# Cross-attention and ternary FFN on one core: order of the first loads, of the first batches' attention and of the first weights

## The chip, the cores and the metric

The kernel runs on one core of one Trainium2 chip. The metric is the time of one execution in microseconds (us). Engines are called as in the profile: PE (TensorE), DVE (VectorE), ACT (ScalarE), POOL (GpSimd) and SP (SyncE, which only issues transfers here). PEld is PE's weight load. Times given as "at 16.50" count from the start of the profiled span.

## The reference

Eight batches of 256 tokens, each token 256 wide, all in float32. Each batch has a context of 120 rows.

```python
x = x + xattn(layernorm(x), ctx)              # scores = xn @ ctx.T, gelu(scores) * scores, @ ctx
h = silu((xn2 @ w1.T) * w1_s) * ((xn2 @ w2.T) * w2_s)     # xn2 = layernorm(x), 256 -> 1024
h = gelu((h @ h1.T) * h1_s)                   # 1024 -> 1024
h = gelu((h @ h2.T) * h2_s)                   # 1024 -> 1024
out = x + (h @ w3.T) * w3_s                   # 1024 -> 256
```

The five weight matrices hold only -1, 0 and 1; the scales are per output column.

## The kernel before

**Tiling.** Tokens are taken in four groups of 512 (t = 0 to 3), two batches (b = 2t, 2t + 1) in each. A batch is two blocks of 128 tokens. Products with ternary weights are run on float32r operands split into a high and a low part, so each appears twice. The two hidden layers use a seven-product scheme on quarter matrices.

**Attention** (`Attention.run`, one call for each batch; batch 0 in two calls of one block each, batch 1 and later in one call of two blocks). Its steps, with their lines: load of x (L212) and of the context (L218) on SP; statistics (L245) and their aggregate (L249) on DVE, for batches 0 and 1 also an addition (L251); the reciprocal root on POOL (L256); the norm (L267 on DVE for batches 0 and 1, L264 on ACT later); transposes on PE (L279) and their copy on ACT (L294); scores on PE (L284); an activation made of L297 (ACT), L298 (DVE), L300 (ACT), L302 (DVE); values on PE (L289); the residual sum (L305, DVE), which SP stores to memory (L420). Then the second layer norm by the same lines, transposes (L279), and the split into the high part (L412, ACT) and the low part (L413, DVE) of the tile xT.

**First FFN layer** (`gated`). For each t, eight groups m of eight products (L443) with the weights w12 and xT, followed by a Silu (L464, ACT) and a product with the other side (L466, DVE). For t = 0 it is run in two halves: first the columns of batch 0 alone (256 wide), then those of batch 1. A group takes its PSUM bank in turn from five: for the first half, bank 1, 2, 3, 4, 0 and so on.

**Weights.** w12 comes in two transfers of 1 MB, issued by POOL (L612), for groups m = 0 to 3 and 4 to 7. They read the key `("first", 0, 0)`, which POOL's root of block 0 of batch 0 writes, so they stand behind it. The hidden layers' weights come later (L355). Loads L379 to L388 check that all weights are exactly representable; a branch at the end takes a general version if not. Only that branch reads `sc_half` and `sc_glu`, which `scales` computes (L619, L620).

**Zero matmuls.** Ahead of everything stand 72 matmuls on zeros (L598, `IDLE = 72`) that write bank 4 and keep PE occupied while the first data arrive. They carry a very low priority. The fourth group of the first layer (m = 3) writes the same bank, so it has to follow all 72.

**Order.** Every step is added to a `Plan` with an engine, a cost, and the keys that it reads (`r`) and writes (`w`). A transfer is added as the issuing step and a step on a model of the DMA engines, with a `lag` until it lands. `chain` puts steps with the same name one behind the other, without a wait between them. The planner computes for each step the longest way to the end, changes a few of these ranks at random for each seed in `PICKS`, and runs a list schedule over the modelled engines. The resulting order is written out: on each engine the instructions then run strictly in that order, each waiting for its own inputs. `hold` adds keys that the first statistics of a batch must wait for.

Of the kernel before, what the change touches and what calls it, by code (L numbers as in the profile page):

```python
# [31 lines left out]
RING = 3  # L32

PICKS = (
    24, 34, 68, 75, 109, 200, 234, 262, 306, 335, 347, 388, 480, 484, 636, 688, 746, 771, 875,
    891, 941, 969, 1092, 1139, 1225, 1283, 1374, 1478, 1505, 1565, 1721, 1792, 1831, 1887, 1946,
    2002, 2028, 2205, 2327, 2434, 2594, 2622, 2698, 2823, 3117, 3852, 3875, 4460, 4870, 4887,
    5689, 8901, 9951, 10170, 10586, 11026, 11996, 12028, 14291, 14841, 14964, 15189, 15290,
    15347, 15386, 15476, 15843, 16236,
)  # L40
ALIGN, ALIGN_W3, ALIGN_RIGHT = 16, 8, 112
IDLE = 72
# [27 lines left out]
class Plan:  # L70
# [6 lines left out]
    def add(self, engine, weight, emit, r=(), w=(), lag=None, early=0.0, chain=None):  # L77
        i, deps = len(self.ops), {}
        if lag is None:
            lag = LAG.get(engine, 0.1)  # L80
        for k in r:
            if k in self.writer:
                deps[self.writer[k]] = True
            self.readers.setdefault(k, []).append(i)
        for k in w:
            if k in self.writer:
                deps[self.writer[k]] = True
            for j in self.readers.pop(k, ()):
                if j != i:
                    deps[j] = True  # L90
            self.writer[k] = i
        if chain is not None:
            if chain in self.last:
                deps.setdefault(self.last[chain], False)
            self.last[chain] = i
        self.ops.append((engine, weight, emit, deps, lag, early))
# [74 lines left out]
PE = 0.12  # L171
# [4 lines left out]
def xattn_ffn_kernel(ctx: ExitStack, tc: tile.TileContext, x, ctx_b, wall, scal, s3, out):  # L176
# [6 lines left out]
    sc = const.tile([P, 32], F32, name="sc")  # L183
# [8 lines left out]
    class Attention:  # L192
# [12 lines left out]
        def load(self, plan, b, pieces):  # L205
            i = b % self.loads
            xv = x[b * S : (b + 1) * S, :].rearrange("(j p) d -> p j d", p=P)

            gate = [("first", b - 3, 0)] if b >= 3 else []

            def load_x(js):
                nc.sync.dma_start(self.xb[i][:, js, :], xv[:, js, :])  # L212

            for js in pieces:
                plan.dma("SP", 0.45, lambda js=js: load_x(js), 0.128 * (js.stop - js.start),
                         lag=(2.2, 3.0, 5.0, 6.0, 6.0)[b] if b < 5 else 4.0, r=gate,
                         w=[("xb", i, j) for j in range(js.start, js.stop)])
            plan.dma("SP", 0.45, lambda: nc.sync.dma_start(self.cb[i], ctx_b[b]), 0.25,  # L218
                     lag=(3.0, 3.5, 5.0, 6.0, 6.0)[b] if b < 5 else 4.0, r=gate, w=[("cb", i)])

        def run(self, plan, b, js, bank, bank_key, x1, x1_key, finish, early, hold=()):


            blocks = range(js.start, js.stop)
            nj = len(blocks)
            n = nj * P
            cols = slice(js.start * P, js.stop * P)
            i, il = b % self.n, b % self.loads
            keys = lambda name: [(name, il if name == "xb" else i, j) for j in blocks]
# [3 lines left out]
            xnT, e, q = self.xnT[i][:, :, cols], self.e[i][:, cols], self.q[i][:, cols]  # L233
# [6 lines left out]
            add = plan.add  # L240
# [46 lines left out]
            def values():  # L287
# [4 lines left out]
            layernorm(xb, keys("xb") + list(hold), "first")  # L292
            add("PE", 0.22 * nj, transposes, keys("xn"), [bank_key])
            add("ACT", act(2 * n), lambda: nc.scalar.copy(xnT, halves), [bank_key], keys("xnT"))  # L294
            add("PE", 0.215 * nj, scores, keys("xnT") + [("cb", il)], [bank_key])

            add("ACT", act(n), lambda: nc.scalar.activation(e, g, AF.Square), [bank_key], keys("e"))  # L297
            add("DVE", dve(n), lambda: nc.vector.scalar_tensor_tensor(  # L298
# [2 lines left out]
                [], keys("q"))  # L301
            add("DVE", dve(n), lambda: nc.vector.scalar_tensor_tensor(  # L302
                e, q, 1.0, e, op0=ALU.add, op1=ALU.mult), keys("q"), keys("e"))
            add("PE", 0.215 * nj, values, keys("e") + [("cb", il)], [bank_key])
            add("DVE", dve(2 * n), lambda: nc.vector.scalar_tensor_tensor(  # L305
                x1, y, 0.5, xb, op0=ALU.mult, op1=ALU.add), [bank_key] + keys("xb"), x1_key)
            layernorm(x1, x1_key, "second")
# [8 lines left out]
    with ExitStack() as es, ExitStack() as wide:  # L316
# [18 lines left out]
        xT = [[early_pool.tile([P, 2, N], F32R, name=f"xT{i}{j}") for i in range(2)] for j in range(2)]  # L335
        later = {}

        plan = Plan()
        add = plan.add
# [63 lines left out]
        def attention(b, pieces, banks, early):  # L403
            t, c, i = b // 2, b % 2, b % att.loads
            att.load(plan, b, pieces)
            for js, bank in zip(pieces, banks):
                cols = slice(c * S + js.start * P, c * S + js.stop * P)
                xkey = [("xT", t % 2, c, j) for j in range(js.start, js.stop)]

                def finish(p, bank_key, n, early, cols=cols, xkey=xkey):  # L410
                    hi, lo = (v[:, :, cols] for v in xT[t % 2])
                    add("ACT", act(2 * n), lambda: nc.scalar.copy(hi, p), r=[bank_key], w=xkey)  # L412
                    add("DVE", dve(2 * n), lambda: nc.vector.tensor_sub(lo, p, hi.bitcast(F32)),  # L413
                        r=[bank_key], w=xkey, early=early)

                x1 = att.xb[i][:, js, :]
                x1_key = [("xb", i, j) for j in range(js.start, js.stop)]
                att.run(plan, b, js, mm[bank], ("mm", bank), x1, x1_key, finish, early,
                        [("xT", 0, 0, j) for j in range(2)] if b in (2, 3) else ())
                plan.dma("SP", 0.45, lambda js=js, x1=x1: nc.sync.dma_start(  # L420
                    x1s[b * S : (b + 1) * S, :].rearrange("(j p) d -> p j d", p=P)[:, js, :], x1),
                    0.13 * (js.stop - js.start), r=x1_key,
                    w=[("x1s", 2 * b + j) for j in range(js.start, js.stop)], lag=4.0)
# [181 lines left out]
        add("ACT", 1.3, lambda: nc.scalar.preload_act_table(AF.Silu), w=["table"], early=400.0)  # L605
        plan.dma("SP", 0.4, lambda: nc.sync.dma_start(sc, scal), 0.016, w=["sc"])
        attention(0, one, (5, 6), 20.0)
        attention(1, both, (7,), 10.0)
        plan.dma("SP", 0.4, lambda: nc.sync.dma_start(s3b, s3.partition_broadcast(P)), 0.13, w=["s3b"])

        def load_w12(c):
            nc.gpsimd.dma_start(w12[:, c : c + 2, :], wall[c : c + 2].rearrange("c p f -> p c f"))  # L612

        for c in (0, 2):
            plan.dma("POOL", 0.8, lambda c=c: load_w12(c), 1.05, r=[("first", 0, 0)],
                     w=[("w12", c), ("w12", c + 1)], chain="weights")

        def scales():
            nc.vector.tensor_scalar_mul(sc_half, sc[:, 0:8], 0.5)  # L619
            nc.vector.tensor_mul(sc_glu, sc_half, sc[:, 8:16])  # L620

        add("DVE", 0.4, scales, r=["sc"], w=["scales"])

        def open_middle():

# [19 lines left out]
        for t in range(1, NT):  # L645
            for b in (2 * t, 2 * t + 1):
                attention(b, both, (5 + (b + 1) % 3,), 6.0)
            for js in (range(2), range(2, 4)) if t < HALVED else (range(4),):
                gated(t, js)
# [8 lines left out]
            later["w3"], wall[20:22].rearrange("c p f -> p c f")), 1.05, r=["later"], w=["w3"],  # L658
            chain="weights", lag=4.0)
        add("ACT", 1.3, lambda: nc.scalar.preload_act_table(AF.Gelu), w=["table"])  # L660
        low, high = (0, 1, 2, 3), (4, 5, 6, 7)
        blocks = [(0, 2, 1, 3), (4, 6, 5, 7)]
        spare = (8, 9)
# [34 lines left out]
    with tc.If(inexact == 0 if FORCE_GENERAL else inexact != 0):  # L698
        with ExitStack() as es:
# [8 lines left out]
            for c in range(NCH):  # L708
                w = wpool.tile([P, 1024], F32, tag=f"g{c}", name=f"g{c}")
# [3 lines left out]
            xT = gbuf.tile([P, 2, S], F32, name="xTg")  # L713
            x1 = gbuf.tile([P, 2, D], F32, name="x1g")
            bank = ppa.tile([P, N], F32, name="gpa")
            for b in range(NB):
                plan = Plan()
# [82 lines left out]
```

## Time and profile before

| | |
|---|---|
| median of 3 runs | 334.45 us (334.01 to 334.62) |
| profiled execution | 334.16 us, its span 332.4 us |
| busy: PE, DVE, ACT, POOL | 324.3, 254.9, 211.6, 54.3 us |
| granted clock of PE, mean | 0.995 |
| transfers | 32.44 MB |

The span runs from the first to the last instruction; the execution has some time around it. The chain that ended last follows the work back from the last instruction, at each step to what released it, or to the instruction ahead on the same engine. The timeline gives, for each line: start, length, engine, line, operation, tiles and shapes, count, and in brackets how long the engine was idle before it and what ended that. A busy PE counts the whole length of a matmul, although the next one starts before its end; the distance between starts is what one costs.

### The profile page before, as it was taken

Reading aid. Unit: us, or ns where it says so; the run is one execution under the profiler, and the core shown is the slowest. Engines: PE = TensorE matmul, PEld = TensorE weight load, DVE = VectorE, ACT = ScalarE, POOL = GpSimd, SP = SyncE. Lnnn points to the kernel's source line nnn. Section 1 sums busy time; section 2 is a strip of 40 time slices with the busy share of each in tenths; the row PEclk is TensorE's granted clock in tenths of the full one; section 3 lists DMA queues with packets and bytes.
Section 4 is the critical chain, followed back from the end, with each engine's and each line's share of the span. In section 5 each row is a group of like instructions: output and inputs, shape, how many; then the busy total and the mean of one; then the engine's idle time right before and its main releaser. Section 6 shows DMA issues by size and latency. Waiting matters only on the chain.

```text
span 332.4 us, 4572 instructions
## 1 busy us (share of the span) xinstructions
PE 324.3 (98%) x1678; PEld 275.7 (83%) x1678; DVE 254.9 (77%) x403; ACT 211.6 (64%) x308; POOL 54.3 (16%) x93
## 2 busy tenths in 40 slices
PE   8999999999999999999999999999999999999992
PEld 6899988888888888888888888888888888899991
DVE  4877999878997549978469999928999426738982
ACT  2367776468398867766769755887865657656500
POOL 4164251020024211111123200141100000000000
PEclk9999999999999999999999999999999999999998
DMA  7989710030079494418849650084500000003432
GB/s 194 330 306 344 230 64 2 32 95 3 0 219 103 44 142 95 98 35 194 217 94 239 63 140 0 0 86 47 59 1 2 0 0 2 0 0 98 128 127 73
DMA packets 22382, 32.44 MB, mean 98 GB/s; under 512 B 1744, under 2 KB 15184, under 8 KB 22352
## 3 DMA queue, kind: packets, MB, share of 16 engines
q0 software_dynamic: 10256, 17.30, 27.7%
q1 hardware_dynamic: 12096, 14.77, 14.3%
q8 instruction: 15, 0.25, 0.3%
q14 instruction: 15, 0.12, 0.1%
HBM read 33.64 MB, written 4.19 MB: 114 GB/s over the span
## 4 chain that ended last, share of the span: by engine, by line
PE 96%; DMA 1%; DVE 1%; SPq 0%; issue 0%; ACT 0%
PE mm L519 61%; PE mm L443 18%; PE mm L565 9%; PE mm L279 2%; PE mm L284 2%; PE mm L289 2%; PE mm L598 2%; DMA xb<-x_d 1%; DVE ln_st L245 0%; DVE o L312 0%; DVE o L313 0%; SPq L218 0%; SPq L212 0%; ACT xT L412 0%; DVE xn L267 0%
## 5 line engine op out<-in xcount | busy, mean ns | idle before, releaser
L519 PE MATMUL mm<-hi,w 128*128 128x512 f32 x448 | 119.7, 389 | 0.0
L519 PE MATMUL mm<-lo,w 128*128 128x512 f32 x448 | 119.7, 389 | 0.0
L492 DVE TENSOR_TENSOR lo<-q,hi 128x1024 fp32r<-128x1024 f32 x72 | 85.7, 1219 | 38.3 <-ACT hi L488 38.2
L519 PEld LDWEIGHTS mm<-hi,w 128*128 128x128 f32 x448 | 84.1, 188 | 17.5
L519 PEld LDWEIGHTS mm<-lo,w 128*128 128x128 f32 x448 | 84.1, 188 | 17.5
L488 ACT CAST hi<-q 128x1024 fp32r<-128x1024 f32 x72 | 72.3, 1046 | 10.1 <-PE mm L565 8.8
L443 PE MATMUL mm<-xT,w 128*128 128x512 f32 (+1 forms) x320 | 64.7, 355 | 0.1
L443 PEld LDWEIGHTS mm<-xT,w 128*128 128x128 f32 x320 | 51.8, 189 | 8.0 <-ACT xT L412 0.4
L538 ACT ACTIVATE q<-q,sc 128x512 f32<-128x512 f32 x48 | 34.1, 721 | 22.2 <-DVE q L534 22.1
L528 ACT COPY q<-mm 128x512 f32<-128x512 f32 x48 | 28.1, 586 | 24.0 <-PE mm L519 23.7
L534 DVE TENSOR_TENSOR q<-q,mm 128x512 f32<-128x512 f32 x48 | 32.5, 682 | 12.0 <-PE mm L519 10.8
L381 POOL DMA_DIRECT2D d<-wall_d x22 | 24.5, 1121 | 101.7 <-ACT d L379 98.5
L511 DVE TENSOR_TENSOR q<-q,q 128x1024 f32<-128x1024 f32 x32 | 38.3, 1216 | 0.0
L464 ACT ACTIVATE q<-mm,sc 128x512 f32<-128x512 f32 (+1 forms) x40 | 24.0, 600 | 16.1 <-PE mm L443 16.1
L466 DVE SCALAR_TENSOR_TENSOR q<-q,sc,mm 128x512 f32<-128x512 f32 (+1 forms) x40 | 25.1, 630 | 4.7 <-ACT q L464 2.4
L379 ACT ACTIVATE d<-w 128x1024 bf16<-128x1024 f32 x22 | 23.2, 1057 | 1.6 <-DVE bad L383 1.6
L363 DVE TENSOR_TENSOR w<-w,w 128x512 fp32r<-128x512 f32 x32 | 20.8, 681 | 0.0
L565 PE MATMUL mm<-w,hi 128*128 128x256 f32 x128 | 20.1, 279 | 0.0
L565 PE MATMUL mm<-w,lo 128*128 128x256 f32 x128 | 20.1, 279 | 0.0
L565 PEld LDWEIGHTS mm<-w,hi 128*128 128x128 f32 x128 | 17.3, 188 | 0.1
L565 PEld LDWEIGHTS mm<-w,lo 128*128 128x128 f32 x128 | 17.2, 188 | 0.0
L538 ACT ACTIVATE q<-mm,sc 128x512 f32<-128x512 f32 x16 | 11.0, 687 | 8.2 <-PE mm L519 8.2
(50 smaller groups left out, 197.7 us busy)
## 6 DMA issues: line engine op xcount, KB each, us to landing
w<-wall_d POOLq DMA_DIRECT2D x11, 1024.0 KB, 7.3
d<-wall_d POOLq DMA_DIRECT2D x22, 256.0 KB, 6.3
w<-wall_d SPq DMA_DIRECT2D x8, 512.0 KB, 3.8
x<-x1s SPq DMA_DIRECT2D x16, 128.0 KB, 2.4
out_d<-o SPq DMA_DIRECT2D x16, 128.0 KB, 1.8
cb<-ctx_d SPq DMA_DIRECT2D x8, 248.0 KB, 4.6
xb<-x_d SPq DMA_DIRECT2D x7, 256.0 KB, 4.4
x1s<-xb SPq DMA_DIRECT2D x7, 256.0 KB, 2.4
```

The lines of the kernel that those rows point to most:

```text
L381: plan.dma("POOL", 0.8, lambda: nc.gpsimd.dma_start(d4, src, accum_op=ALU.add), 1.04, w=[("d", i)], lag=8.0)
L443: nc.tensor.matmul(sides[side], lhsT=w12[:, m // 2, (((m % 2) * 2 + side) * 2 + k) * P :][:, :P], rhs=xT[t % 2][i][:, k, cols], start=firs ...
L464: add("ACT", act(n, 1), lambda o=o, b0=b0, m=m: nc.scalar.activation(o, b0, AF.Silu, scale=sc[:, m : m + 1]), r=[("mm", banks[0]), "sc", " ...
L466: add("DVE", dve(n) + 0.05, lambda o=o, b1=b1, m=m: nc.vector.scalar_tensor_tensor(o, o, sc[:, 8 + m : 9 + m], b1, op0=ALU.mult, op1=ALU.m ...
L488: nc.scalar.copy(slot_views(i)[0][:, ms], q[src][:, ms])
L492: nc.vector.tensor_sub(l[:, ms], q[src][:, ms], h[:, ms].bitcast(F32))
L511: add("DVE", dve(1024), lambda ms=ms: nc.vector.tensor_tensor(q[into][:, ms], q[x][:, ms], q[y][:, ms], op=ALU.subtract), r=q_keys(x, ms) ...
L519: nc.tensor.matmul(mm[bank], lhsT=w[:, m, k, :], rhs=part[:, k, :], start=(p in OPENS and kind == 0 and k == 0), stop=(p in CLOSES and kin ...
L528: add("ACT", act(512), lambda: nc.scalar.copy(q[i][:, m], mm[bank]), r=[key], w=[("q", i, m)])
L534: add("DVE", dve(512), lambda: nc.vector.tensor_tensor(o(), o(), mm[bank], op=ALU.add), r=[key], w=[("q", i, m)])
L538: add("ACT", act(512, 1), lambda: nc.scalar.activation(o(), src(), AF.Gelu, scale=sc[:, col : col + 1]), r=["sc", "table"] + ([] if p in a ...
L565: nc.tensor.matmul(mm[banks[j]][:, :D], lhsT=part[:, k, j * P : (j + 1) * P], rhs=later["w3"][:, r, k * D : (k + 1) * D], start=(r == 0 an ...
```

## The change

- The loads of x and context of batches 0 and 1 get the chain `loads`: both blocks of batch 0, its context, then batch 1. Their modelled lags become shorter.
- `run` takes a second list, `hold_values`, which is added to what the values step reads. The statistics of batch 1 are held until POOL's root of block 1 of batch 0 (`("first", 0, 1)`), its values until block 1's part of xT is written.
- The two loads of w12 read `("first", 0, 1)` instead of `("first", 0, 0)`.
- `scales` reads the key `later`, written where the tiles of the hidden layers' second pool are opened, and is added after the loading of the Gelu table.
- The planner's PE cost of scores and values is doubled, and the list `PICKS` is another, of 61 seeds instead of 68.

```diff
 PICKS = (
-    24, 34, 68, 75, 109, 200, 234, 262, 306, 335, 347, 388, 480, 484, 636, 688, 746, 771, 875,
...
+    24, 34, 68, 74, 98, 161, 181, 212, 226, 262, 369, 407, 428, 476, 490, 556, 637, 719, 750,
...
             gate = [("first", b - 3, 0)] if b >= 3 else []
+            chain = "loads" if b < 2 else None
...
                 plan.dma("SP", 0.45, lambda js=js: load_x(js), 0.128 * (js.stop - js.start),
-                         lag=(2.2, 3.0, 5.0, 6.0, 6.0)[b] if b < 5 else 4.0, r=gate,
+                         lag=(1.5, 2.5, 5.0, 6.0, 6.0)[b] if b < 5 else 4.0, r=gate, chain=chain,
                          w=[("xb", i, j) for j in range(js.start, js.stop)])
             plan.dma("SP", 0.45, lambda: nc.sync.dma_start(self.cb[i], ctx_b[b]), 0.25,
-                     lag=(3.0, 3.5, 5.0, 6.0, 6.0)[b] if b < 5 else 4.0, r=gate, w=[("cb", i)])
-
-        def run(self, plan, b, js, bank, bank_key, x1, x1_key, finish, early, hold=()):
+                     lag=(1.8, 3.0, 5.0, 6.0, 6.0)[b] if b < 5 else 4.0, r=gate, chain=chain, w=[("cb", i)])
+
+        def run(self, plan, b, js, bank, bank_key, x1, x1_key, finish, early, hold=(), hold_values=()):
...
-            add("PE", 0.215 * nj, scores, keys("xnT") + [("cb", il)], [bank_key])
+            add("PE", 0.43 * nj, scores, keys("xnT") + [("cb", il)], [bank_key])
...
-            add("PE", 0.215 * nj, values, keys("e") + [("cb", il)], [bank_key])
+            add("PE", 0.43 * nj, values, keys("e") + [("cb", il)] + list(hold_values), [bank_key])
...
-                        [("xT", 0, 0, j) for j in range(2)] if b in (2, 3) else ())
+                        {1: [("first", 0, 1)], 2: [("xT", 0, 0, 0), ("xT", 0, 0, 1)],
+                         3: [("xT", 0, 0, 0), ("xT", 0, 0, 1)]}.get(b, ()),
+                        [("xT", 0, 0, 1)] if b == 1 else ())
...
         for c in (0, 2):
-            plan.dma("POOL", 0.8, lambda c=c: load_w12(c), 1.05, r=[("first", 0, 0)],
+            plan.dma("POOL", 0.8, lambda c=c: load_w12(c), 1.05, r=[("first", 0, 1)],
                      w=[("w12", c), ("w12", c + 1)], chain="weights")
...
-        add("DVE", 0.4, scales, r=["sc"], w=["scales"])
...
         add("ACT", 1.3, lambda: nc.scalar.preload_act_table(AF.Gelu), w=["table"])
+        add("DVE", 0.4, scales, r=["sc", "later"], w=["scales"])
```

## The prediction

> **What bounds the kernel now.** I read the page first, then the chain of waits that ended last, then the timeline of the first 17 us, then the landings of the weights. From the page:
>
> ```profile
> span 332.4 us, 4572 instructions
> PE 324.3 (98%) x1678; PEld 275.7 (83%) x1678; DVE 254.9 (77%) x403; ACT 211.6 (64%) x308; POOL 54.3 (16%) x93
> PE 96%; DMA 1%; DVE 1%; SPq 0%; issue 0%; ACT 0%
> L598 PE MATMUL mm<-zeros 128*128 128x256 bf16 x72 | 11.5, 307 | 1.2 <-DVE zeros L593 1.2
> ```
>
> TensorE (PE) is busy 324.3 of 332.4 us. Of the 8.1 us that are left, 1.15 lie before its first instruction and 6.7 behind its last product (325.64 to 332.4), so almost nothing lies between. Among its work are 72 matmuls on zeros (L598), which compute nothing. Now the chain in order of time (start, length):
>
> ```profile
> 1.65 2.57 DMA xb<-x_d
> 4.25 0.44 DVE ln_st L245
> 5.08 0.33 DVE xn L267
> 5.90 0.76 PE mm L598 x7
> 12.55 1.97 PE mm L598 x18
> 15.82 0.23 PE mm L279 x2
> 16.07 0.38 ACT xT L412
> 16.50 4.32 PE mm L443 x32
> 92.64 203.12 PE mm L519 x896
> 295.75 29.88 PE mm L565 x256
> ```
>
> The first real products (L443) start at 16.50, released by the second block of batch 0. From there on PE issues without a pause worth naming: 203.12 us for 896 products are 0.2267 each, from end to end of the hidden layers. Before 16.50 the zero matmuls fill whatever the attention leaves free, at 0.76/7 = 0.109 us each. That decides how the change must be priced. All 72 are still issued, since the fourth group of first-layer products writes bank 4 behind the last of them. An earlier attention chain therefore doesn't shorten PE's queue; it only exchanges what stands where in it. **The end moves by two things alone: waits of PE that vanish, and waits of PE that appear.**
>
> The timeline shows where batch 0 loses time, and the waits of the weight loads (PEld) what there is to win:
>
> ```profile
> 4.30 0.90 POOL L612 DMA_DIRECT2D w<-wall_d  x1
> 5.21 0.62 POOL L256 TENSOR_TENSOR ln_rs<-ln_ve,eps_exp 128x1 f32<-128x1 f32 x1
> 5.45 0.20 PEld L279 LDWEIGHTS mm<-ident,xn 128*128 128x128 f32 x2 [0.43 <-DVE xn L267]
> 6.30 0.75 DVE L245 BATCH_NORM_STATS2 ln_st<-xb 128x6 f32<-128x256 f32 x2 [0.90 <-DMA xb<-x_d]
> 7.42 0.20 PEld L279 LDWEIGHTS mm<-ident,xn 128*128 128x128 f32 x2 [0.28 <-DVE xn L267]
> 8.33 0.17 DVE L619 TENSOR_SCALAR sc_half<-sc 128x8 f32<-128x8 f32 x1 [0.60 <-DMA sc<-scal_d]
> 16.50 0.30 PEld L443 LDWEIGHTS mm<-xT,w 128*128 128x128 f32 x2 [0.41 <-ACT xT L412]
> 16.96 3.66 PEld L443 LDWEIGHTS mm<-xT,w 128*128 128x128 f32 x30 [0.16 <-DVE xT L413]
> ```
>
> **Gains: 0.6 us taken, 0 to 1.3 possible.** Four waits of PE touch the edits: 0.43 + 0.28 + 0.41 + 0.16 = 1.28 us. More can't be won ahead of the products.
> - x of block 1 is issued second, not third on SP: at 1.19 instead of 1.65, so it lands at 3.6 to 3.8 instead of 4.22. The context of batch 0 slips one place, from a landing at 3.9 to some 4.5; scores need it at 6.4. Free; without that cover it would cost what it lands late.
> - Statistics of batch 1 no longer stand ahead of block 1's norm: DVE waits 0.90 and works 0.75 less before it, of which about 1.1 us counted (POOL's root was done at 5.83, the norm began at 6.97). Moved are two L245, two L249 and L251, 1.2 us of DVE in all, into DVE time that is idle later.
> - The scales, L619 and L620 with 0.60 of waiting, leave DVE's queue: 0.9 us on block 0's path, some 0.2 of it on block 1's, whose L298 came at 9.67 behind block 0's. Both go behind the layer tiles, where DVE has room; only the branch not taken reads them.
> - Values of batch 1 (four L289, 0.87 us of PE) go behind block 1's transposed tile. PE work moved, not removed: 0.
> - The planner's cost of scores and values doubles, its lags of the first loads shrink, and its list of nudges is another: everything is ordered afresh, no instruction is added. The gated stage changes between attention and L443 some twenty times, with 0.05 to 0.2 us lost at each; I put the new order at 0, bounds -0.5 and +1.
>
> By these, block 1's chain would be ready near 13.3: from a landing at 3.7, its 12.3 us from 4.2 to 16.5, less 1.1 in front of the norm, 0.2 behind the scales, 0.65 where L249 of block 1 (13.34) stood behind batch 1's L298, and 0.7 behind batch 1's values. So PE would have most of these 1.28 us back, were it not for the next edit. I take half, 0.6, because an order fixed in advance always leaves some.
>
> **The price: the weights wait for the second root.** Both loads of the first-layer weights (L612) now stand behind POOL's root of block 1 instead of block 0. POOL then issues root, root, load, load. The second root ended at 5.83; with the earlier landing I expect 5.2 to 5.7, so the first load starts at 5.2 to 5.8, not 4.30. Queued behind the two loads (0.90 + 0.76) is batch 1's root, which nothing urgent awaits. The landings, from the answer on L612's line, and the queues' answers for 4 to 8 and 8 to 9 us:
>
> ```profile
> DMA to landing us min/median/max: 10.1/11.3/12.5
> q1 hardware_dynamic: 984, 1.05, 92.0%
> q0 software_dynamic: 12, 0.05, 32.9%
> ```
>
> The shorter is the first: it lands at 4.30 + 10.1 = 14.4, the other at 5.80 + 12.5 = 18.3. The old products came at 16.50, 2.1 us behind the first; the second half is needed 3.84 us of products later, also 2 us behind. That margin is spent from both ends.
> - Landing: later by the whole shift (0.9 to 1.5), or by nothing, if the loads already under way decide: the weights' queue (q0) moved its first 0.05 MB only after 8, while SP's queue (q1) had the engines. Bounds 14.4 and 15.9; I take 15.3, since between 11 and 15 us q0 moves a steady 0.3 MB per us, and a later start has nothing to catch up with.
> - Arrival of PE: 16.50 less 0.87 (values moved behind) less 0.6 is 15.0 if all 72 zero matmuls stay in front; 13.3 if the planner lets the first three product groups overtake as many as the chain allows. I take 14.0, which is nine of them behind.
> - Wait: 15.3 - 14.0 = 1.3 us, bounds 0 and 15.9 - 13.3 = 2.6.
>
> The Trainium skill, page "DMA: Bandwidth & Descriptors", section "Queues, rings and completion order", says that each DMA engine takes turns between its queues packet by packet. By that rule the late load is not pushed back by a backlog, and shifts by its own delay, as I took it; the 3.9 us in which q0 moved nothing speak against it for the start-up.
>
> **Sum.** +1.3 - 0.6 = +0.7 us. The profiled execution took 334.16 with a span of 332.4, 1.8 lying around it; the median is 334.45, 0.3 above, a difference the change doesn't touch. On the median: 334.45 + 0.7 = 335.1, 0.2% slower. About 0.2%, 0.67 us, is what a measurement of this kernel can tell from no change.
>
> **Rivals.**
> 1. *The weights are there in time.* The landing stays near 14.4 or the zero matmuls keep the products back past 15. Then only the vanished waits count: -0.6, at most -1.28, hence 333.85, down to 333.2. For it: all 72 stood ahead of the products before. Against: the new holds take away what delayed the chain in the planner too, so there is less to keep the products behind. This is the best case; far more than 0.4% isn't to be had from a PE queue of the same length.
> 2. *Batch 1 starves the second half.* Its values now wait until block 1's tile is finished. Before, its values ended at 15.7 and its tile (L413) at 23.4, while the first half's products ended at 27.1: 3.7 us to spare. If values slip to 18.5 or later by standing behind several product groups, with the wait for the weights ahead, PE waits at the second half. It decides beyond 3.7 us of slip less the products' own shift; two microseconds beyond it gives 334.45 + 2 = 336.5. Against: the planner sees this chain and can put the values behind the first group.
> 3. *The wait cools PE.* At its start PE issues zeros at 4.16/20 = 0.21 us each, until 4.75, that is for 3.6 us; later at 0.109. If a wait at the upper bound brought the slow rate back for as long, products worth 1.8 us would take 3.6: +1.8 on top of the wait of 2.6, less 0.6: 334.45 + 3.8 = 338.25. Against: PE never paused so long here. The Trainium skill's page "TensorE: Matmul & The Clock Gate", section "What's actually happening", has PE fall to half rate after an idle window of about 3.4 us; by that rule a wait of 1.3 us costs nothing more.
> 4. *The new order opens stalls in the hidden layers*, which have none to lose now (0.2267 us a product throughout): 0.5 to 3 us, say 336.0.
>
> **How the numbers follow.** Forecast (334.5 to 335.9) 0.50; rival 1 0.25; rival 2 0.10; rival 3 0.03; rival 4 0.12. Half of the forecast's own spread lies above 335.1, that is 0.25 slower and 0.25 within 0.2%; rival 1 gives 0.16 faster and 0.09 same; the rest 0.25 slower. Faster 0.16, same 0.34, slower 0.50. The range takes in rival 1 to its end (333.2) and rivals 2 and 4 up to 337.0.
>
> **What would show it.** Right: x of block 1 lands before 3.9; L619 gone from the first 20 us; block 1's norm within 0.3 us of its root; L612 first issued after 5.1; zero matmuls between groups of L443; an idle of about 1.3 us before the first L443, released by the DMA of w. Wrong: L443 starting before 15 with no idle, the first load landing by 14.5, or a span whose excess lies behind 93 us.

## The result

| | before | after |
|---|---|---|
| median | 334.37 us (333.51 to 334.62, 8 runs) | 333.24 us (332.94 to 333.90, 8 runs) |
| profiled execution, its span | 334.16, 332.4 us | 333.42, 331.6 us |

The ratio is 0.9975, interval 0.9965 to 0.9985: the change gains 0.5 to 1.2 us, where 335.1, a loss of 0.7, was forecast. It is rival 1 at its far end: the weights are there in time.

From the page of the kernel after:

```profile
span 331.6 us, 4584 instructions
PE 323.5 (98%) x1678; PEld 275.8 (83%) x1678; DVE 256.2 (77%) x403; ACT 212.1 (64%) x308; POOL 53.9 (16%) x93
PE 96%; DMA 1%; DVE 1%; POOL 0%; SPq 0%; issue 0%
```

PE is still what bounds it, with the same 1678 matmuls. Now its chain of waits in order of time (start, length); L600 are the zeros and L445 the first-layer products after the change, L521 the hidden layers, L567 the output:

```profile
1.19 2.35 DMA xb<-x_d
5.43 0.47 PE mm L279 x2
13.60 1.20 PE mm L600 x11
14.80 0.86 PE mm L289 x4
15.66 2.97 PE mm L445 x24
18.63 0.89 PE mm L600 x8
91.94 197.68 PE mm L521 x872
296.02 28.95 PE mm L567 x248
```

The hidden layers begin at 91.94 instead of 92.64, and PE's last product ends at 324.97 instead of 325.64. So 0.7 of the 0.74 us by which the two executions differ is won ahead of 92 us. Nothing behind it changed: 6.6 us lie behind the last product (6.7 before), and PE waits nowhere between.

The step that the forecast turned on is in the timeline, in the landing of the weights (L614), and in the queues for 4 to 8 and 9 to 10 us (packets, MB, share):

```profile
4.35 1.11 POOL L256 TENSOR_TENSOR ln_rs<-ln_ve,eps_exp 128x1 f32<-128x1 f32 x2 [3.04 <-DVE ln_mv L249]
5.42 1.63 POOL L614 DMA_DIRECT2D w<-wall_d  x2
5.42 0.24 PEld L279 LDWEIGHTS mm<-ident,xn 128*128 128x128 f32 x2 [0.94 <-DVE xn L267]
13.63 0.37 ACT L412 CAST xT<-mm 128x256 fp32r<-128x256 f32 x1 [0.29 <-PE mm L279]
14.04 0.42 DVE L413 TENSOR_TENSOR xT<-mm,xT 128x256 fp32r<-128x256 f32 x1 [0.23 <-ACT xT L412]
14.63 1.03 PE L289 MATMUL mm<-cb,ge 120*128 120x256 f32 x4
15.50 2.93 PEld L445 LDWEIGHTS mm<-xT,w 128*128 128x128 f32 x24 [0.24 <-issue]
18.48 1.05 PE L600 MATMUL mm<-zeros 128*128 128x256 bf16 x8
```
```profile
DMA to landing us min/median/max: 10.0/11.4/12.8
q1 hardware_dynamic: 989, 1.08, 85.3%
q0 software_dynamic: 6, 0.02, 7.3%
```

The first load is issued at 5.42, behind both roots, 1.12 later than before. Its queue (q0) moves its first bytes only after 9 us (after 8 before), and it lands at 15.4, 1.0 later: the landing shifts with the issue. The tile of block 1 is ready at 14.46, but PE then issues the values of batch 1 (L289, 14.63 to 15.50) and arrives at the products at 15.5. Weights and PE meet within 0.1 us: PE issues its first product 0.03 us later than its queue alone would have it.

In two more profiles of the change (parts 2 and 4 below) the weights landed at 15.28 and 14.78. In the second of them PE lost nothing. In the first it was done with the values at 15.22 (14.36 and four at 0.215) and lost 0.20:

```profile
14.36 1.03 PE L289 MATMUL mm<-cb,ge 120*128 120x256 f32 x4
15.39 2.93 PEld L445 LDWEIGHTS mm<-xT,w 128*128 128x128 f32 x24 [0.40 <-issue]
15.42 3.11 PE L445 MATMUL mm<-xT,w 128*128 128x256 f32 x24
```

The profile names no releaser for it, but the weight load starts 0.11 behind the landing, 0.10 in the profile above, and 0.10 in part 3, where the wait for the weights is plain. So the wait that was forecast is most likely there, at 0 to 0.2 us and not at 1.3.

Adding up the distances between the starts of PE's matmuls:

| us | before | after |
|---|---|---|
| first product starts | 16.50 | 15.53 |
| zero matmuls ahead of it | 72 | 64 |
| PE waits ahead of it | 0.89 | 0.77 |
| lost at changes of stage behind it, up to 92 us | 3.00 | 2.64 |

Of the 0.97 by which the products start earlier, 8 x 0.109 = 0.87 is only work put behind them. The rest of the gain is 0.1 of waits, 0.36 of small losses behind the first product (of which 0.32 is the wait for the first tile's two parts, which stood inside the first group before), and some 0.2 in gaps too small to name.

### The profile page after: what moved, and what is told of

It is laid out like the page before. It is cut to its first block, busy times and chain, and to the rows that moved or that the text cites. A ratio compares the mean times of both kernels' runs of the same rounds, so it can differ in the third digit from the quotient of the medians.

```text
span 331.6 us, 4584 instructions
## 1 busy us (share of the span) xinstructions
PE 323.5 (98%) x1678; PEld 275.8 (83%) x1678; DVE 256.2 (77%) x403; ACT 212.1 (64%) x308; POOL 53.9 (16%) x93
## 3 DMA queue, kind: packets, MB, share of 16 engines
q1 hardware_dynamic: 12096, 14.77, 14.5%
## 4 chain that ended last, share of the span: by engine, by line
PE 96%; DMA 1%; DVE 1%; POOL 0%; SPq 0%; issue 0%
PE mm L521 61%; PE mm L445 18%; PE mm L567 9%; PE mm L279 2%; PE mm L284 2%; PE mm L289 2%; PE mm L600 2%; DMA xb<-x_d 1%; POOL ln_rs L256 0%; DVE o L312 0%; DVE ln_st L245 0%; DVE o L313 0%; DVE xn L267 0%; SPq L212 0%; DVE ln_mv L249 0%
## 5 line engine op out<-in xcount | busy, mean ns | idle before, releaser
L521 PE MATMUL mm<-hi,w 128*128 128x512 f32 x448 | 119.9, 390 | 0.0
L521 PE MATMUL mm<-lo,w 128*128 128x512 f32 x448 | 119.8, 389 | 0.0
L521 PEld LDWEIGHTS mm<-lo,w 128*128 128x128 f32 x448 | 84.1, 188 | 17.4
L521 PEld LDWEIGHTS mm<-hi,w 128*128 128x128 f32 x448 | 84.0, 188 | 17.4
L445 PE MATMUL mm<-xT,w 128*128 128x512 f32 (+1 forms) x320 | 64.8, 356 | 0.0
L445 PEld LDWEIGHTS mm<-xT,w 128*128 128x128 f32 x320 | 51.9, 189 | 7.7 <-issue 0.2
L567 PE MATMUL mm<-w,hi 128*128 128x256 f32 x128 | 20.1, 279 | 0.0
L567 PE MATMUL mm<-w,lo 128*128 128x256 f32 x128 | 20.1, 279 | 0.0
L567 PEld LDWEIGHTS mm<-w,hi 128*128 128x128 f32 x128 | 17.3, 188 | 0.2
L567 PEld LDWEIGHTS mm<-w,lo 128*128 128x128 f32 x128 | 17.2, 188 | 0.0
```

Of the source, the lines that this page charges most:

```text
L445: nc.tensor.matmul(sides[side], lhsT=w12[:, m // 2, (((m % 2) * 2 + side) * 2 + k) * P :][:, :P], rhs=xT[t % 2][i][:, k, cols], start=firs ...
L521: nc.tensor.matmul(mm[bank], lhsT=w[:, m, k, :], rhs=part[:, k, :], start=(p in OPENS and kind == 0 and k == 0), stop=(p in CLOSES and kin ...
L567: nc.tensor.matmul(mm[banks[j]][:, :D], lhsT=part[:, k, j * P : (j + 1) * P], rhs=later["w3"][:, r, k * D : (k + 1) * D], start=(r == 0 an ...
```

## The experiments

Every kernel below runs the order that the planner made for the change or for the kernel before, spliced by hand where the diff shows it. The diffs list steps in the order of their engine and are not lines of the kernel. Ratios are to the kernel before on the same chip. A run's median has 11 or 12 executions.

**1. Parts of the change undone**

The hold on the weights undone:

```diff
 POOL: root of block 0
+POOL: load w12, c = 0
 POOL: root of block 1
-POOL: load w12, c = 0
 POOL: load w12, c = 2
```

> The changed kernel in its own order on every engine; only POOL's first weight load stands between the two roots again, as in the kernel before. Theory A (PE's queue is the bound, and the hold on the weights bought nothing and cost nothing): the first load lands at 14.2 to 14.6 instead of 15.42, PE still reaches its first product at 15.5, time within 0.3 us of the changed kernel (333.0 to 333.5). Theory B (holding the weights is what lets the tokens and the roots come early): block 1's root and norm slip by 0.3 us or more, time 333.5 to 334.4.

334.01 us, ratio 0.9989 (0.9973 to 1.0006). Undoing what the prediction charged as a price made nothing faster. The load landed at 14.3, but block 1's root came at 5.59 instead of 4.91.

The eight zeros behind the third product group left out of the change, and the last eight left out of the kernel before (they compute nothing):

```diff
-PE: zeros 64 to 71
```

> The changed kernel without the eight zero matmuls that stand behind its third product group; everything else in the same order. Theory A (every matmul in PE's queue behind the first product counts in full): 8 x 0.109 = 0.87 us less than the changed kernel, 332.4. Theory B (behind the first product another thing sets the pace, the second weight load or batch 1's tile): no gain, 333.2, and a wait of PE shows before the fifth product group.

> The kernel before without its last eight zero matmuls, which all stand ahead of the first product. Theory A (ahead of the products block 1's chain was the bound too, so the zeros there are partly free): PE waits instead, 0.2 to 0.5 us gained, 333.9 to 334.2. Theory B (PE's queue alone counts there as well): 0.87 us gained, 333.5.

332.95 us (0.9956, 0.9942 to 0.9970) and 334.00 (0.9987, 0.9974 to 1.0000). By these medians neither pays the full 0.87, though both intervals reach it. In the change without the eight, two waits for batch 2's norm appear a little behind the place of the zeros (timeline):

```profile
22.02 0.20 PEld L279 LDWEIGHTS mm<-ident,xn 128*128 128x128 f32 x2 [0.28 <-ACT xn L264]
22.51 0.64 PEld L279 LDWEIGHTS mm<-ident,xn 128*128 128x128 f32 x6 [0.29 <-ACT xn L264]
```

Both waits stand in the profile of part 5's first kernel too, which leaves out the same eight. So a zero matmul is partly a filler of a wait and partly a cost. This was the fastest version measured (once, on one chip; part 5 gives a reason for doubt).

Batch 1's values put behind the first product group, which is where the prediction had them:

```diff
-PE: values of batch 1 (L289 x4)
 PE: products of m = 0 (L445 x8)
+PE: values of batch 1 (L289 x4)
```

> The changed kernel with batch 1's values behind the first product group instead of ahead of it; nothing else moved. Theory A (in the changed kernel these 0.87 us of values filled the wait for the late weights, which is where the forecast failed): PE stands ready at 14.65, waits until the landing at 15.4, and the time rises by 0.7 to 0.9 us to 334.0. Theory B (the place of the values doesn't matter, there was no wait to fill): within 0.3 us of the changed kernel, 333.2.

333.56 us (0.9969, 0.9951 to 0.9986), no loss beside the change's 0.9975. In its profile PE came to the products at 14.69 and the weights had landed at 14.5. So PE's arrival was 0.7 later than the 14.0 of the sum, and the landing 0.8 earlier than its 15.3.

**2. Parts of the change made alone, on the kernel before**

The change once more; block 1's tokens ahead of the context on SP, with batch 1's statistics behind block 1's norm on DVE; batch 1's values held; the change's named moves without that of the weights, in the order of before:

> The changed kernel as it is, as the measure for the others on the same chip. Both theories: 333.2, that is 1.1 us under the kernel before. It also tells whether the 0.8 us by which the kernel with the early weights stood above the changed kernel holds on one more chip.

```diff
 SP: x of block 0
+SP: x of block 1
 SP: context of batch 0
-SP: x of block 1
...
-DVE: statistics of batch 1
 DVE: norm of block 1
+DVE: statistics of batch 1
```

> The kernel before in its own order, with two steps moved: the second block's tokens are issued ahead of batch 0's context on SP, and batch 1's statistics stand behind block 1's norm on DVE. Theory A (the gain is waits of PE that vanish): the waits ahead of the two first transposes, 0.31 + 0.17 us and the 0.06 behind each, go; 333.7 to 333.9. Theory B (the start is slack, the gain comes from the new order further on): within 0.2 us of before.

```diff
-PE: values of batch 1
 PE: second transposes of block 1
+PE: values of batch 1
```

> The kernel before in its own order, with one step moved: batch 1's values on PE behind block 1's second transposes, as the change holds them. Theory A: the wait of 0.30 us ahead of the first product and the 0.2 to 0.3 inside the first group go, 333.8 to 334.0. Theory B: within 0.2 us of before.

Both of these together, and the scales moved as in the change:

```diff
-DVE: scales (L619, L620)
...
 ACT: loading of the Gelu table
+DVE: scales (L619, L620)
```

> The kernel before in its own order with the moves of the other two and the scales behind the Gelu table; the weights stay where they were, and the planner's new order is left out. Theory A (these moves are the whole gain): the sum of the two, 0.8 to 1.1 us, 333.3 to 333.6, all of it ahead of 17 us. Theory B (the new order or the held weights carry part of it): above 333.9.

The change again: 333.36 (0.9984, 0.9974 to 0.9993). Tokens alone: 333.65 (0.9986, 0.9977 to 0.9995); its PE waits only 0.30 ahead of the first product. Values held alone: 334.34 (1.0005, 0.9995 to 1.0015). The moves without the weights: 333.97 (1.0001, 0.9990 to 1.0012). The last two had a flaw: the residual sum of batch 1 (L305), which needs those values, still stood ahead of the low part of block 1's tile on DVE, and PE waited for it. From the timeline with the values held alone:

```profile
17.32 2.81 PEld L443 LDWEIGHTS mm<-xT,w 128*128 128x128 f32 x23 [0.75 <-DVE xT L413]
```

The moves without the weights again, with that sum moved along:

```diff
-DVE: residual sum of batch 1 (L305)
 DVE: low part of block 1's tile (L413)
+DVE: residual sum of batch 1 (L305)
```

> The kernel before in its own order with the tokens first, batch 1's statistics held, the scales moved and batch 1's values held, this time with batch 1's residual sum moved behind block 1's low part on DVE too; on the older attempt that sum stood ahead of it and made PE wait 0.71 us. Theory A (the moves are the gain of the change): no wait above 0.3 us ahead of or in the first product group, 0.5 to 0.9 us below before. Theory B (the new order carries it): within 0.3 us of before.

334.06 (0.9994, 0.9984 to 1.0004). The wait is gone from its profile, but the gain isn't there. Its profile has other waits instead, 0.35 us at the transposes at 19.6 and 0.27 at 21.6 (by the starts of the matmuls). By the medians the tokens' move is worth most by itself in the order of before, and the held values add nothing to it; the intervals overlap.

**3. The forecast's own mechanism, provoked**

The values behind the first group and zeros 53 to 63 left out as well, so that PE arrives early; with the weights held, and with the first load between the roots:

```diff
-PE: zeros 53 to 63
-PE: values of batch 1 (L289 x4)
 PE: products of m = 0 (L445 x8)
+PE: values of batch 1 (L289 x4)
```

> The changed kernel with the fillers of the wait taken away: batch 1's values behind the first product group, and the eleven zero matmuls ahead of them left out. Theory A (the late weights are a price that the zeros and the values had covered): PE stands ready with block 1's tile at 14.4 to 14.6 and waits for the landing at 15.3 to 15.5; with the values now behind, 0.6 to 0.9 us above the changed kernel, although eleven matmuls are gone. Theory B (no price, the weights would be there): first product at 14.6, 0.1 to 0.3 us below the changed kernel.

> As the kernel with the emptied queue, with POOL's first weight load back between the two roots. Theory A: the load lands at 14.2 to 14.6, the first product starts at 14.6 to 15.0, and the time is 0.5 to 0.9 us below that kernel. Theory B (block 1's root, held up 0.7 us by the load's issue, sets the start instead): the tile is ready later by as much, and the time within 0.3 us of that kernel.

The first products in the two timelines, weights held and then early:

```profile
16.34 1.19 PE L445 MATMUL mm<-xT,w 128*128 128x256 f32 x8 [2.41 <-DMA w<-wall_d]
```
```profile
14.44 1.44 PE L445 MATMUL mm<-xT,w 128*128 128x256 f32 x8 [0.46 <-ACT xT L412]
```

Here is the wait that was forecast: PE was done at 13.9, the weights landed at 5.8 + 10.4 = 16.2. Of the 2.41 us the last 2.0 are the weights' own, since the high part of block 1's tile was ready at 14.34. With the early load PE waits 0.46, for that tile. Yet the medians are 333.61 (0.9976, 0.9965 to 0.9987) and 333.64 (0.9984, 0.9974 to 0.9994). The profiled execution with the wait was the slowest of its kernel (335.09; the others from 332.61), so the wait is probably shorter in most; how long it is in those can't be seen. In that execution block 1's tokens landed at 3.90, against 3.2 to 3.6 in all but one of the other profiles of this order, and the roots and the load came late with them. The version with the early load loses elsewhere: its chain of waits names the tokens of batch 4, whose statistics stand on DVE ahead of batch 1's second norm.

```profile
6.03 11.96 DMA xb<-x_d
18.37 1.06 DVE ln_st L245 x3
21.46 0.77 PE mm L279 x4
```

A version meant to be the best of all, with the early load, block 1's statistics behind block 0's aggregate on DVE, and the last 19 zeros left out:

```diff
-PE: zeros 53 to 71
...
-DVE: statistics of block 1
 DVE: aggregate of block 0
+DVE: statistics of block 1
```

> A version meant to be faster than both: the changed kernel with block 1's statistics behind block 0's aggregate on DVE (so that block 0 no longer waits for block 1's tokens), the first weight load between the two roots, and the last nineteen zero matmuls left out. Theory A (PE's queue up to the point where the data are there is what counts): first product at 14.7 to 15.2, eight matmuls fewer behind it, 1.0 to 1.6 us below the changed kernel. Theory B (activation work of batch 2 sets the pace behind the start, as the waits for L264 showed when eight were dropped): 0.3 to 0.6 us below.

333.78 us (0.9980, 0.9971 to 0.9988), no better than the change. Batch 4's tokens landed at 18.2, and PE waited 0.9 for the norm on DVE and 0.4 for that on ACT. Its start did improve: PE's first transposes came at 4.82, where the three profiles of the change have 5.12 to 5.43. So block 1's statistics, which stand ahead of block 0's aggregate in the change, are what holds block 0 there.

**4. The hold on the weights by itself**

On one chip: the hold alone, the hold with the tokens' move, the change, and the change without the hold (the diff of part 1 for the last; the reverse move for the first).

```diff
 POOL: root of block 0
-POOL: load w12, c = 0
 POOL: root of block 1
+POOL: load w12, c = 0
 POOL: load w12, c = 2
```

> The kernel before with one move: on POOL both loads of w12 stand behind the root of block 1 of batch 0 (as in the change), all else as before. Theory A (the hold is a small gain by itself): POOL reaches block 1's root 0.9 us earlier only if block 1's tokens are there, and in this order they are not (its norm on DVE waits for them), so the root moves little; the load lands about 15.3, still ahead of PE's arrival at 16.2 to 16.5: 334.0 to 334.3 beside 334.35. Theory B (the hold costs, as the prediction said, wherever the load is on the path): the load lands a microsecond later, PE would wait only if it landed after 16.2; spread up, 334.4 to 335.0.

> The kernel before with two moves: block 1's tokens ahead of the context on SP with batch 1's statistics behind block 1's norm on DVE, and both loads of w12 behind block 1's root on POOL. Theory A (these two together are the change's gain; the held values, the scales and the rest are nothing): block 1's root follows its tokens at once, 333.2 to 333.5 beside 334.35 for before, within 0.2 of the change itself. Theory B (the tokens alone are the gain and the hold adds nothing): as the tokens alone, 333.8 to 334.0.

> The change as it is, for the comparison on this chip: 333.2 to 333.6 by both theories.

> The change with one part undone: the first load of w12 stands between the two roots again, as before. Theory A (the hold on the weights is itself a gain in this order, since the issue of 0.9 us no longer stands ahead of block 1's root): 333.8 to 334.1, a third to two thirds of a microsecond over the change on this chip. Theory B (the hold is neutral): within 0.2 of the change. The prediction's own term (a price of 0 to 2.6): faster than the change, 332 to 333.3.

The hold alone: 334.38 (1.0005, 0.9996 to 1.0015). With the tokens: 333.95 (0.9992, 0.9983 to 1.0001). The change: 333.20 (0.9977, 0.9963 to 0.9991). The change without the hold: 333.98 (0.9989, 0.9980 to 0.9998), as in part 1. So in the order of before the hold shows no effect, with the tokens or without; in the order after, the medians put it at a gain of 0.8 us on this chip, the ratios at 0.4, with intervals that overlap. Ten of the change's twelve executions were faster than the fastest of the eleven without the hold. So the hold is a gain here and no price.

The profiles show where, with a caution: the execution profiled without the hold was its kernel's slowest (334.89), the one with it nearly the fastest (333.03). First the timeline of the change without the hold, POOL, PE and DVE:

```profile
4.95 0.90 POOL L614 DMA_DIRECT2D w<-wall_d  x1
5.86 0.59 POOL L256 TENSOR_TENSOR ln_rs<-ln_ve,eps_exp 128x1 f32<-128x1 f32 x1
6.96 0.44 PE L279 MATMUL mm<-ident,xn 128*128 128x128 f32 x2 [0.59 <-DVE xn L267]
19.07 1.41 DVE L245 BATCH_NORM_STATS2 ln_st<-xb 128x6 f32<-128x256 f32 x4 [1.66 <-DMA xb<-x_d]
22.50 0.76 PE L279 MATMUL mm<-ident,xn 128*128 128x128 f32 x4 [0.47 <-DVE xn L267]
```

Then the timeline of the change on this chip at the same places:

```profile
4.04 1.11 POOL L256 TENSOR_TENSOR ln_rs<-ln_ve,eps_exp 128x1 f32<-128x1 f32 x2 [2.73 <-DVE ln_mv L249]
5.83 0.38 PE L279 MATMUL mm<-ident,xn 128*128 128x128 f32 x2
16.48 1.41 DVE L245 BATCH_NORM_STATS2 ln_st<-xb 128x6 f32<-128x256 f32 x4 [0.18 <-DMA xb<-x_d]
```

Without the hold, the 0.90 us in which POOL issues the load stand ahead of block 1's root: the root starts 1.26 us later than it does with the hold (5.86 against 4.60). Of that, 0.37 is block 1's tokens, which landed at 3.60 in this execution and at 3.23 in the other; the rest is the issue. PE, which takes block 1's transposes four zeros behind block 0's in this order, waits 0.59 for them. And batch 4's tokens land 2.6 us later, at 19.05, hold up DVE, and PE waits a second time at 22.5. This second wait is not in part 1's profile of the same kernel, where these tokens landed at 17.57.

**5. Is the second place a cost?** Batch 4's statistics moved on DVE behind batch 1's second norm, in the fastest version and in the change without the hold:

```diff
-DVE: statistics of batch 4 (L245 x2), aggregate (L249 x2)
 DVE: second statistics, aggregate and norm of batch 1
+DVE: statistics of batch 4 (L245 x2), aggregate (L249 x2)
```

> The change with two more edits: the eight zero matmuls behind the third product group are left out (they compute nothing), and on DVE the first statistics of batch 4 stand behind the second norm of batch 1 instead of ahead of its second statistics. Theory A (batch 4's tokens, landing 16.5 to 19, hold batch 1's second norm and with it PE's transposes at 22): the wait of PE near 22 goes, 332.6 to 332.9, a tenth or three under the change with the zeros left out alone (332.95 beside a before of 334.33). Theory B (batch 4's statistics are harmless where they are, or are late themselves once moved): 332.9 to 333.4.

> The change with the first load of w12 back between the two roots, and batch 4's first statistics on DVE behind batch 1's second norm. Theory A (undoing the hold costs in two places: block 1's root behind the issue, and batch 4's tokens late behind the weights, with batch 1's norm queued behind them): the wait of 0.64 to 0.71 near 22.5 goes, that near 7 stays; 333.5 to 333.8, between the change (333.2) and the change without the hold (334.0). Theory B (the tokens' delay does not matter, only the root does): 333.9 to 334.1, as without the move.

333.93 us (0.9988, 0.9978 to 0.9998) and 334.16 (1.0002, 0.9993 to 1.0011): theory A missed both times. In the second kernel the wait at 22.5 did go. In the first the two waits near 22 stayed (at 20.3 and 20.8): they are for batch 2's norm on ACT, and in the profile of the fastest version batch 4's tokens had landed by 12.3, so theory A had taken the wrong cause for them. In both kernels the statistics now stood ahead of a later step on DVE, and PE waited there. From the two timelines, the fastest version first:

```profile
26.20 0.73 PEld L289 LDWEIGHTS mm<-cb,ge 120*128 120x128 f32 x4 [0.50 <-DVE ge L302]
```
```profile
26.34 0.73 PEld L289 LDWEIGHTS mm<-cb,ge 120*128 120x128 f32 x4 [0.29 <-DVE ge L302]
```

So the tokens' delay is shown as a wait in the trace, and not as a cost in time. The first kernel's median stands 1.0 above that of the fastest version, on another chip, and this wait is only half of it: how much of that version's lead is its own stays open.

What is left to explain the difference that the hold makes is the wait for block 1's norm near 7 us. By the starts of PE's matmuls it was 0.76 in this profile and in that of part 4, but only 0.2 in part 1's and in that of part 3's early load. PE's clock goes with this: full rate came at 4.4 and 5.2 us in the first two, and at 6.6 and 6.4 in the others, where the four zeros between the transposes took 0.85 us instead of 0.44 and covered most of the wait. That this wait is the whole difference is likely, and not settled.

## Why the prediction was wrong

**The step that failed: the arrival of PE, 14.0.** It came at 15.5. Two terms of it were wrong.
- "Less 0.87 (values moved behind)". They were not moved behind the products. A hold only says from when a step may run; block 1's tile was ready at 14.46, and the planner put the values right there, ahead of the first product. The list of held keys was read as an order.
- "Less 0.6" for vanished waits. Ahead of the first product they fell from 0.89 to 0.77. The later waits went, as forecast, but the first one grew from 0.37 to 0.67. Three zeros fewer stand ahead of it, and block 0's norm starts no earlier than before (4.96 against 5.00): DVE now does block 1's statistics ahead of block 0's aggregate, so block 0 waits for block 1's tokens. With that undone PE's first transposes came at 4.82 (part 3). The new order was put at zero; this is part of what it cost.

The chain of block 1, put near 13.3, was late as well: the high part of its tile was ready at 14.00. That did not decide, since PE came later still.

With 15.5 in place of 14.0, the prediction's own sum gives no wait, and rival 1. The products did come past 15, as that rival's second condition says, but batch 1's values kept them back and not the zeros: with the values behind, PE came at 14.69 (part 1).

**The price itself.** The mechanism exists: with PE at 13.9 the weights cost 2.0 us in one execution (part 3), and in the change itself most likely 0 to 0.2. Landing (15.4 against 15.3), issue (5.42, within 5.2 to 5.8) and the eight zeros behind (nine forecast) were as worked out. But even with the values truly behind, PE and weights met within 0.2 us. The landing varies as much as the price: in the seven profiles of the new order with the hold it lay between 14.5 and 16.2. And the term had the wrong sign in its surroundings: it counted what stands behind the loads on POOL (batch 1's root), and not what the loads no longer stand ahead of, block 1's root. In the old order that root was held by its tokens anyway (it starts at 5.21, and at 5.30 with the hold alone); in the new one the tokens are there.

**The gain.** 0.74 between the profiled executions, 0.84 by the ratio, where 0.6 was taken and 1.28 was the most. Right in size, though only 0.4 of it lies in the four waits that the sum named: 0.1 ahead of the products and the 0.3 inside the first group. The rest is smaller losses that the sum did not name, so the size of the gain is in part luck.

**What was right.** PE's queue is what sets the end, so block 1's tile, ready 2.4 us earlier (14.46 against 16.9), bought only 0.7. Block 1's tokens landed at 3.54 (before 3.9 was said). L619 is gone from the start, the hidden layers and the tail did not move, and rivals 2, 3 and 4 did not happen. Rival 3 fails even with the long wait of part 3: the eight products behind 2.41 us of idling took 1.19 us, as elsewhere (1.20).

**What stays open.** How the 0.84 divides. Tokens alone gave 0.9986, the change 0.9975 to 0.9984 on three chips, the change without the hold 0.9989 twice; the intervals are as wide as the differences. By the medians the hold pays only together with the new order, so the parts don't add. Scales and lags were not tried alone.

## What to carry to other kernels

Before charging a late transfer, find the consumer's arrival in the queue of its engine, and read a hold as an earliest time and not as a place: the planner may slip other work in front, as it did here. Price the issuing instruction at both ends of its move, by what comes to stand behind it and by what it no longer blocks. In a queue full of filler, a chain that is ready 2.4 us earlier is worth only the waits that vanish, and each wait removed shows the next (here batch 2's norm, then batch 4's tokens).

## What the runs showed of the hardware

**Transfers of tokens pay for the weights issued ahead of them.** The tokens of batches 3 and 4 were issued at 5.04 and 6.03 to 6.3 us in every kernel. In the nine profiles whose first weights went out at 5.1 to 5.9 they landed 5.8 to 6.9 and 6.3 to 11.4 us later; in the eleven where they went out at 4.2 to 4.95, 7.7 to 11.4 and 11.5 to 13.6 us later. In the pair that differs by the hold alone (the kernel before and part 4's first) 10.5 and 12.4 us became 6.3 and 8.2. The first load itself took 9.4 to 10.4 us in the nine and 9.1 to 10.3 in the eleven. The Trainium skill, page "DMA: Bandwidth & Descriptors", section "Queues, rings and completion order", has each DMA engine take turns between its queues packet by packet; the runs agree in that both queues move data in the same microsecond (from 10 to 11 us after the change, 0.19 MB on the weights' queue and 0.18 MB on SP's).

**PE's clock comes up at a different time in each execution.** The zero matmuls at the start are 0.214 us apart and then 0.109. The change turned at 5.54, 3.94 and 4.91 in three profiles, other kernels between 4.2 and 9.5. Nine profiles in which PE waited nowhere ahead of the turn have it between 3.94 and 6.41; the latest, at 9.53, followed a wait of 1.0 us at 4.75, the longest that any of them had ahead of its turn. That was the version without the eight zeros: the half rate cost 3.58 us there, against 1.4 to 1.8 in the three of the change, and that execution took 335.23 where its kernel's median is 332.95. The Trainium skill, page "TensorE: Matmul & The Clock Gate", section "What's actually happening", calls the window that decides it free-running and the count of slow matmuls run-variable; the spread here agrees, but 9.5 is more than two of its windows of 3.4 us behind PE's start at 1.15. So one profile of such a kernel is one draw: effects under half a microsecond are for medians to tell.
